# Half-height products turned into full-height ones: the last 64 hidden features of a transformer block's down projection

## The chip, the core and the metric

The kernel runs on one core of a Trainium2 chip. The metric is the device time of one execution in microseconds, the median of several runs. The profile is one separately taken execution of the same kernel; its times are counted from the start of its span.

## What is computed

A transformer block with adaptive layer norm, in float32, for two sequences of 1024 tokens with 256 features. The attention has 16 heads of 128 with rotary positions and a causal mask; the feed-forward part is gated, with 704 hidden features and weights given as integers with a scale per output.

```python
mod = (_silu(c) @ wmod).reshape(2, 6, 1, -1)
sa, ca, ga, sb, cb, gb = (mod[:, n] for n in range(6))
h = _layernorm(x) * (1 + ca) + sa
x = x + ga * attention(h)
h = _layernorm(x) * (1 + cb) + sb
gate = _silu(qlinear(h, wq_gate, s_gate))
up = qlinear(h, wq_up, s_up)
x = x + gb * qlinear(gate * up, wq_down, s_down)
```

(ga and gb are first kept at least 0.25 away from zero.) The change concerns the last line: the sum over the 704 hidden features.

## The kernel before

TensorE multiplies a stationary operand by a moving one; the dimension that is summed lies on the partitions, up to 128 of them, which are the rows of its array. 704 = 5 x 128 + 64, so the hidden features make NF = 6 chunks, five full ones and one of 64.

**Stages.** The kernel goes through 32 units (2 sequences x 16 heads). In each, the eight query tiles are scored, exponentiated, turned and multiplied with the values, and the projections of the next head are mixed in. The order is written out by hand in the loop at L753 and in `extras`, and the engines take their instructions in that order. The feed-forward part is done in four blocks of 512 tokens, named by sequence and half: (0,0), (0,1), (1,0), (1,1). The products of block (0,0) are mixed into the last attention unit, those of (0,1) into what is left of attention after it; the rest follows in the order of L813 to L830.

**One block.** `hidden(b, blk, c)` (L534) makes chunk c of the hidden features, transposed: features on the partitions, tokens along. It takes two products of TensorE (gate and up, L547), a Silu on ScalarE and a multiplication on VectorE, which writes the tile gT_b,blk (128 partitions x 6 chunks x 512 tokens). For the last chunk one product gives 64 gate features and 64 up features, and `last_gate_up` (L564) multiplies them. Its result is stored in two halves by token: of each 256 tokens, the first 128 (j even) go to partitions 0 to 63, and the other 128 (j odd) to partitions 64 to 127 (L573). The other half of the partitions of that chunk is written by nobody. `wq_down` is laid out to match: its last 64 rows are there twice, on partitions 0 to 63 and on 64 to 127 (L885).

`down(b, blk)` (L583) sums over the features. For each of four token tiles j there is an accumulator pd in PSUM, five products over the full chunks (`chunks`, L606) and one over the last chunk (`halves`, L596), which takes the 64 partitions that hold tile j. Then VectorE adds the residual (L622), and the DMA queue stores the rows (L623). In the first three blocks the halves come after all chunks; in the last block (1,1), whose chunk 5 is made first, they come before them. There the fourth token tile is split into two accumulators of 128 columns (pd and pd_11r).

**Buffers.** The gT tiles come from the pool `fpool` with two buffers: (0,0) and (1,0) use one, (0,1) and (1,1) the other. Before them, the same buffers hold the transposed layer norm of sequence 0, which GpSimd reads in `ln_shift` (L249) in the unit before the last. A tile's first writer waits until the last reader of the buffer's tile before it is done. The gate and up products after attention use the PSUM pool `ps_sc` with two buffers, each freed by the multiplication that reads it (L573, L581).

**GpSimd** does the rotary multiplications (L401, L407), the folding of the gates into the output weights (L339 to L343), the bias (L357) and the shifts of L249 during attention, and a few fills at the start. It has no work in the feed-forward blocks.

Of the kernel before, what the change touches and what calls it, by code (L numbers as in the profile page):

```python
# [11 lines left out]
F32 = mybir.dt.float32  # L12
# [5 lines left out]
P = 128  # L18
B, S, D = 2, 1024, 256
H, DH = 16, 128  # L20
HID = 704
# [4 lines left out]
NF = (HID + P - 1) // P  # L26
FULL = (HID // P) * P
QB = 512
# [9 lines left out]
def adaln_block(ctx: ExitStack, tc: tile.TileContext, a, cos_d, sin_d, out):  # L38
    nc = tc.nc
# [5 lines left out]
    fpool = pool("f", 2)  # L45
# [11 lines left out]
    cols = const.tile([P, 3 * H], F32, name="cols")  # L57
# [206 lines left out]
    wdT = [const.tile([P, NF, D], F32, name=f"wdT{b}") for b in range(B)]  # L264
# [240 lines left out]
    def bank(name):  # L505

        pool, tag = banks[turn[0] % 4]
        turn[0] += 1
        return pool.tile([P, 512], F32, tag=tag, name=name)
# [16 lines left out]
    h2s, gTs = {}, {}  # L526
# [6 lines left out]

    def hidden(b, blk, c, late=True, first=None, hold=False):  # L534
        if c == 0 if first is None else first:
            gTs[b, blk] = fpool.tile([P, NF, QB], F32, tag="f", name=f"gT_{b}{blk}")
        last = c == NF - 1
        if late:
            pg = ps_sc.tile([P, S], F32, tag="sc", name=f"pgu_{b}{blk}{c}")
            pgs = [pg[:, ts(j, QB)] for j in range(2)]  # L540
        else:
            pgs = [
                ps_a.tile([P, 512], F32, tag="a", name=f"pgu_{b}{blk}{c}{j}") for j in range(2 - last)
            ]
        for pg, n in zip(pgs, ("gate",) if last else ("gate", "up")):
            for k in range(KC):
                nc.tensor.matmul(  # L547
                    pg,
                    wT["last"][:, k, :] if last else wT[n][:, k, ts(c, P)],
                    h2s[b, blk][:, k, :],  # L550
                    start=(k == 0),
                    stop=(k == KC - 1),
                )
        sg = ppool.tile([P, QB], F32, tag="p", name=f"sg_{b}{blk}{c}")

        rest = (last_gate_up if last else full_gate_up)(b, blk, c, sg, pgs)
        if hold:
            owed.append(rest)
        else:
            rest()  # L560
# [22 lines left out]
    def down(b, blk):  # L583

        end = (b, blk) == (1, 1)
        pds = [bank(f"pd_{b}{blk}{j}") for j in range(4)]

        parts = [(j, pds[j], slice(0, D)) for j in range(4)]
        if end:
            rest = ps_sc.tile([P, S], F32, tag="sc", name=f"pd_{b}{blk}r")  # L590
            parts[3:] = [(3, pds[3], slice(0, P)), (3, rest, slice(P, D))]

        def halves():
            for j, pd, cols in parts:
                half = ts(j % 2, HID - FULL)
                nc.tensor.matmul(  # L596
                    pd[:, cols],
                    gTs[b, blk][half, NF - 1, ts(j, P)],
                    wdT[b][half, NF - 1, cols],
                    start=end,  # L600
                    stop=not end,
                )

        def chunks(j, pd, cols):
            for c in range(NF - 1):
                nc.tensor.matmul(  # L606
                    pd[:, cols],
                    gTs[b, blk][:, c, ts(j, P)],
                    wdT[b][:, c, cols],
                    start=(c == 0 and not end),  # L610
                    stop=(c == NF - 2 and end),
                )

        def store(j, pd, cols):
            t = blk * 4 + j
            if cols.start == 0:
                if (b, blk) == (0, 0):
                    yos[t] = rot.tile([P, D], F32, tag="r1", name=f"yo_{b}{t}")
                else:
                    yos[t] = xnp.tile([P, D], F32, tag="xn", name=f"yo_{b}{t}")  # L620
            yo = yos[t]
            nc.vector.tensor_tensor(yo[:, cols], pd[:, cols], x[b][:, t, cols], ALU.add)  # L622
            nc.sync.dma_start(out[b, ts(t, P), cols], yo[:, cols])  # L623

        yos = {}
        if end:

            halves()
            for part in parts:
                chunks(*part)  # L630
                store(*part)
            return
        for part in parts:
            chunks(*part)
        halves()
        for part in parts:
            store(*part)
# [62 lines left out]
    with tc.manual_schedule():  # L700
# [52 lines left out]
        for n, u in enumerate(units):  # L753
            b, g, h = u
# [4 lines left out]
            for i in range(NT):  # L759
# [20 lines left out]
                if not nxt and i in filler:  # L780
                    hidden(0, 0, filler.index(i), late=False, hold=True)
# [13 lines left out]
        for c in range(4):  # L795
            hidden(0, 1, c, hold=True)
            if c == 0:
                values(u, 0, 0, 4)
            for _ in range(2 + (c == 3)):
                shared_out(s, late=True)  # L800
                s += 1
            owed.pop()()
# [4 lines left out]
        values(u, 1, 0, 8)  # L807
        ln_scale(1, "b", 0)
        hidden(0, 1, 4)
        for t in range(4, NT):  # L810
            project_out(u, t, late=True)
# [85 lines left out]
```

## Time and profile before

| | |
|---|---|
| median of 3 runs | 1075.6 us (1075.38 to 1075.73) |
| profiled execution | 1076.84 us, of which the span is 1075.1 us |
| TensorE busy | 1070.5 us, 3529 records |
| VectorE / ScalarE / GpSimd busy | 655.1 / 507.7 / 396.1 us |
| granted TensorE clock | 1.00 |

| where in the profiled execution | us from the start |
|---|---|
| first product of the hidden layer written to gT_00 (L581) | 929.07 |
| last product of block (0,1)'s hidden layer, then layer norm | 991.03 to 993.62 |
| down product (0,0): full chunks, then halves | 993.62, 1002.35 |
| down product (0,1) | 1018.13, 1026.85 |
| down product (1,0) | 1045.38, 1054.10 |
| down product (1,1): halves, then full chunks | 1062.23, 1063.31 |
| last output addition | 1072.32 |

A line of the timeline gives the start, the length from the first record's start to the last one's end, the engine, the line of the code, the operation, the result and operands, the shape (for TensorE: rows * columns of the array, then rows x columns of what is streamed) and the number of records that were merged. PE is TensorE, PEld its weight loads, DVE VectorE, ACT ScalarE, POOL GpSimd, SPq the DMA queue. A float32 product leaves two records. The ends of TensorE's records are modelled, and so overlap with the next start; distances between starts are the safer measure.

### The profile page before, as it was taken

The page shows a single profiled execution, that of the slowest core. Times are in us where ns is not written, and L with a number is a line of the kernel's source. Part 1 is how long each engine was busy: PE and PEld are TensorE (multiplying, and loading weights), DVE is VectorE, ACT ScalarE, POOL GpSimd, SP SyncE. Part 2 cuts the span into 40 slices and gives each one's busy share as a digit, 9 for nine tenths or more (in the row PEclk, how much of TensorE's full clock was granted, in tenths as well). Part 3 has the DMA queues.
Part 4 walks back from the last instruction along what each step waited for, and adds up shares of the span by engine and source line. Part 5 has one row for each costly group of instructions (what it writes and reads, how often), then busy time and mean ns, then how long its engine had stood idle before and what let it go on. Part 6 is the DMA issues. An engine that isn't in the chain of part 4 may idle for free.

```text
span 1075.1 us, 12364 instructions
## 1 busy us (share of the span) xinstructions
PE 1070.5 (100%) x3529; PEld 641.4 (60%) x3529; DVE 655.1 (61%) x1423; ACT 507.7 (47%) x956; POOL 396.1 (37%) x364
## 2 busy tenths in 40 slices
PE   9999999999999999999999999999999999999998
PEld 5656555666666655555666656655555666555656
DVE  5656665666767776665666566666677765544421
ACT  4654544554445544544554444444454554562110
POOL 3825353534343343754332443324343433100000
PEclk9999999999999999999999999999999999999999
DMA  6465655657565555565554656454555556432001
GB/s 218 96 161 126 161 119 135 164 127 181 118 152 112 142 117 134 122 149 126 112 148 109 147 113 155 101 139 99 139 114 126 143 128 137 103 69 49 20 20 40
DMA packets 66656, 130.99 MB, mean 122 GB/s; under 512 B 18806, under 2 KB 22010, under 8 KB 66588
## 3 DMA queue, kind: packets, MB, share of 16 engines
q1 hardware_dynamic: 64804, 125.78, 49.4%
q10 hardware_dynamic: 1736, 4.29, 1.2%
q8 instruction: 29, 0.48, 0.2%
q14 instruction: 39, 0.32, 0.1%
q0 software_dynamic: 48, 0.13, 0.1%
HBM read 25.26 MB, written 2.10 MB: 25 GB/s over the span
## 4 chain that ended last, share of the span: by engine, by line
PE 99%; DMA 0%; DVE 0%; SPq 0%; issue 0%
PE po L492 23%; PE ps L431 23%; PE pv L370 10%; PE pq L388 10%; PE py L518 10%; PE pk L388 10%; PE pgu L547 7%; PE pd L606 3%; PE pm L125 1%; DMA wmod<-in_wmod 0%; PE pd L596 0%; PE ptx_a L218 0%; PE pg L149 0%; PE ptx_b L218 0%; PE pd_11r L606 0%; DVE x L521 0%
## 5 line engine op out<-in xcount | busy, mean ns | idle before, releaser
L451 ACT ACTIVATE p<-ps,nmax 128x128 f32<-128x128 f32 (+7 forms) x256 | 189.8, 741 | 342.7 <-DVE nmax L434 342.3
L431 PE MATMUL ps<-kT,qT 128*128 128x512 f32 (+3 forms) x768 | 289.5, 486 | 0.0
L434 DVE CUSTOM_DVE_ANT_0 ps<-ps,mask 128x128 f32<-128x128 f32 (+7 forms) x256 | 195.5, 764 | 114.5 <-PE ps L431 113.6
L492 PE MATMUL po<-pT,v 128*128 128x512 f32 (+3 forms) x768 | 263.7, 486 | 0.1
L521 DVE SCALAR_TENSOR_TENSOR x<-py,rden,x 128x256 f32<-128x256 f32 x256 | 122.7, 481 | 220.6 <-PE py L518 216.8
L492 PEld LDWEIGHTS po<-pT,v 128*128 128x128 f32 x768 | 145.7, 190 | 123.9 <-issue 92.8
L401 POOL TENSOR_TENSOR r_q<-r_q,sin_t 128x512 f32<-128x512 f32 x64 | 81.9, 1280 | 364.5 <-ACT r_q L400 348.9
L465 DVE STREAM_TRANSPOSE t<-p 128x128 f32<-128x128 f32 (+7 forms) x256 | 198.2, 774 | 3.6 <-DMA pT<-t 1.8
L431 PEld LDWEIGHTS ps<-kT,qT 128*128 128x128 f32 x768 | 145.7, 190 | 77.6 <-issue 64.1
L518 PE MATMUL py<-wo,o 128*128 128x256 f32 x512 | 151.2, 380 | 0.0
L518 PEld LDWEIGHTS py<-wo,o 128*128 128x128 f32 x512 | 92.6, 190 | 77.6 <-issue 53.1
L370 PE MATMUL pv<-wv,hT 128*128 128x256 f32 x512 | 121.1, 379 | 0.0
L388 PE MATMUL pq<-hT,wq 128*128 128x512 f32 x256 | 120.5, 593 | 0.0
L388 PE MATMUL pk<-hT,wk 128*128 128x512 f32 x256 | 120.3, 592 | 0.0
L370 PEld LDWEIGHTS pv<-wv,hT 128*128 128x128 f32 x512 | 94.8, 190 | 19.5 <-issue 1.3
L401 POOL TENSOR_TENSOR r_k<-r_k,sin_t 128x512 f32<-128x512 f32 x64 | 81.5, 1273 | 64.4 <-ACT r_k L400 64.4
L407 POOL TENSOR_TENSOR kT<-kT,r_k 128x512 f32<-128x512 f32 x64 | 81.2, 1269 | 55.8 <-DVE kT L404 41.1
L400 ACT ACTIVATE r_q<-pq,cols 64x512 f32<-64x512 f32 x128 | 87.4, 683 | 22.3 <-PE pq L388 19.8
L407 POOL TENSOR_TENSOR qT<-qT,r_q 128x512 f32<-128x512 f32 x64 | 83.7, 1308 | 33.9 <-DVE qT L404 29.7
L400 ACT ACTIVATE r_k<-pk,cols 64x512 f32<-64x512 f32 x128 | 87.4, 683 | 6.4 <-PE pk L388 1.0
L388 PEld LDWEIGHTS pk<-hT,wk 128*128 128x128 f32 x256 | 48.6, 190 | 48.0 <-issue 44.2
L388 PEld LDWEIGHTS pq<-hT,wq 128*128 128x128 f32 x256 | 46.2, 190 | 33.1 <-issue 30.6
(96 smaller groups left out, 691.3 us busy)
## 6 DMA issues: line engine op xcount, KB each, us to landing
pT<-t SPq DMA_DIRECT2D x512, 128.0 KB, 2.4
pT<-t SPq DMA_DIRECT2D x512, 64.0 KB, 2.0
wq<-in_Wq SPq DMA_DIRECT2D x16, 256.0 KB, 3.0
wk<-in_Wk SPq DMA_DIRECT2D x16, 256.0 KB, 4.1
wv<-in_Wv SPq DMA_DIRECT2D x16, 256.0 KB, 4.1
wo<-in_Wo SPq DMA_DIRECT2D x16, 256.0 KB, 2.9
out<-yo SPq DMA_DIRECT2D x15, 128.0 KB, 1.8
wmod<-in_wmod SPq DMA_DIRECT2D x4, 256.0 KB, 5.5
```

What stands on the lines that cost most here:

```text
L370: nc.tensor.matmul(pv[:, ts(j, HG * DH)], hT[b, n][:, k, ts(r, P)], weights[b, g]["v"][:, k, :], start=(k == 0), stop=(k == KC - 1),)
L388: nc.tensor.matmul(pq, weights[b, g][s][:, k, ts(h, DH)], hT[b, n][:, k, :], start=(k == 0), stop=(k == KC - 1),)
L400: nc.scalar.activation(r1[to], pq[of], AF.Identity, bias=cols[of, c : c + 1])
L401: nc.gpsimd.tensor_tensor(r1, r1, sin_t[:, sl], ALU.mult)
L407: nc.gpsimd.tensor_tensor(dst[:, sl], dst[:, sl], r1, ALU.add)
L431: nc.tensor.matmul(ps[:, c:e], qT[:, ts(i, P)], kT[:, c:e], start=True, stop=True)
L434: nc.vector.tensor_tensor_reduce(ps[:, :L], ps[:, :L], mask[:, NT - 1 - i :, :].rearrange("p t k -> p (t k)"), -SCALE, FLT_MAX, ALU.add, A ...
L451: nc.scalar.activation(p[:, :L], ps[:, :L], AF.Exp, bias=nmax, scale=-1.0, accum_out=dens[u][:, i : i + 1])
L465: nc.vector.transpose(t32[blk][:, :, j, : i + 1, :].rearrange("p c k b -> p k c b"), p[:, : (i + 1) * P].rearrange("p (k c a) -> p k c a", ...
L492: nc.tensor.matmul(po[:, off * P :], vs[b, g][:, k, ts(h, DH)], pT[:, off:, :, k, :], start=(k == 0), stop=(k == last),)
L518: nc.tensor.matmul(py[:, :D], outs[u][:, ts(t, P)], weights[b, g]["o"][:, h, :], start=True, stop=True)
L521: nc.vector.scalar_tensor_tensor(x[b][:, t, :], py[:, :D], rdens[u][:, t : t + 1], x[b][:, t, :], ALU.mult, ALU.add)
```

## The change

The last chunk's products no longer take the 64 partitions of their token tile but all 128. So that the other 64 add nothing, GpSimd writes zeros there: two fills for each gT tile, ahead of its first product. They clear partitions 64 to 127 of the even token tiles and 0 to 63 of the odd ones. What VectorE writes stays the same, and so do the weights, of which both copies are now read in each product. The number of products stays the same; their sum differs by nothing but products with zero.

```diff
     def hidden(b, blk, c, late=True, first=None, hold=False):
         if c == 0 if first is None else first:
-            gTs[b, blk] = fpool.tile([P, NF, QB], F32, tag="f", name=f"gT_{b}{blk}")
+            gT = gTs[b, blk] = fpool.tile([P, NF, QB], F32, tag="f", name=f"gT_{b}{blk}")
+
+            for j, rows_ in enumerate((slice(HID - FULL, P), slice(0, HID - FULL))):
+                nc.gpsimd.memset(
+                    gT[rows_, NF - 1, :].rearrange("p (t j q) -> p t j q", j=2, q=P)[:, :, j, :], 0.0
+                )
...
         def halves():
             for j, pd, cols in parts:
-                half = ts(j % 2, HID - FULL)
                 nc.tensor.matmul(
                     pd[:, cols],
-                    gTs[b, blk][half, NF - 1, ts(j, P)],
-                    wdT[b][half, NF - 1, cols],
+                    gTs[b, blk][:, NF - 1, ts(j, P)],
+                    wdT[b][:, NF - 1, cols],
                     start=end,
                     stop=not end,
                 )
```

## The prediction

> **What bounds the kernel now.** I read the page's busy table first, then the chain of waits for the stretch after attention, then TensorE's timeline around one down product, record by record, and last GpSimd's timeline. The busy table and the slices say which engine matters:
>
> ```profile
> PE 1070.5 (100%) x3529; PEld 641.4 (60%) x3529; DVE 655.1 (61%) x1423; ACT 507.7 (47%) x956; POOL 396.1 (37%) x364
> ...
> PE 99%; DMA 0%; DVE 0%; SPq 0%; issue 0%
> ```
>
> TensorE is busy in 1070.5 of 1075.1 us, and 99% of the chain that ended last is TensorE. So a nanosecond added to or taken from TensorE's stream is one of the end. The edited products are four places in the last 82 us; this is how TensorE's timeline lists one of them and its neighbours (start, length, records):
>
> ```profile
> 993.62 8.80 PE L606 MATMUL pd<-wdT,gT 128*128 128x256 f32 x40
> 1002.35 1.14 PE L596 MATMUL pd<-wdT,gT 64*128 64x256 f32 x8
> 1003.41 1.98 PE L547 MATMUL pgu<-h,wgateT 128*128 128x512 f32 x4
> 1005.23 1.88 PE L547 MATMUL pgu<-h,wupT 128*128 128x512 f32 x4
> ```
>
> Each fp32 product leaves two records, so the four half products (L596) are 8 records, and the twenty full ones (L606) 40. The lengths overlap, because the ends are modelled; what counts is the distance between starts. Cutting the window down to single records gives these starts (the first is the last L606 record, then four pairs of half-height records, then the first gate products):
>
> ```profile
> 1002.04 0.38 PE L606 MATMUL pd<-wdT,gT 128*128 128x256 f32 x1
> 1002.35 0.49 PE L596 MATMUL pd<-wdT,gT 64*128 64x256 f32 x2
> 1002.67 0.38 PE L596 MATMUL pd<-wdT,gT 64*128 64x256 f32 x2
> ...
> 1003.10 0.38 PE L596 MATMUL pd<-wdT,gT 64*128 64x256 f32 x2
> 1003.41 0.70 PE L547 MATMUL pgu<-h,wgateT 128*128 128x512 f32 x1
> 1003.95 0.59 PE L547 MATMUL pgu<-h,wgateT 128*128 128x512 f32 x1
> 1004.38 0.59 PE L547 MATMUL pgu<-h,wgateT 128*128 128x512 f32 x1
> ```
>
> Two things are to be seen. The half-height records come two at a time (x2 in one line at one start; a third pair starts at 1002.88): a product on rows 0 to 63 and one on rows 64 to 127 run together. And the steps are not even: 0.31, 0.32, 0.21, 0.22, 0.31, then 0.54 where the next is 0.43. The normal step of a 128x256 record is (1002.04 - 993.62)/39 = 0.216, and of a 128x512 record 0.43. So each change between full and half height costs about 0.1 on two steps: 0.09 + 0.10 going in and 0.10 + 0.11 coming out, 0.40 us for the four half products.
>
> **What the Trainium skill says.** "TensorEngine Tiling (Array Packing)", Key Properties, says that different tiles run in parallel, and that changing the tiling mode, as against the tile, drains TensorE. This trace agrees with both: four shared starts, and four stretched steps of 0.09 to 0.11 us. "TensorE: Matmul & The Clock Gate", in the section on LDWEIGHTS, says that a weight load's time depends on the columns and not on the rows; here 186 ns at 64 rows and 190 at 128, so the load itself won't grow. "SBUF — State Buffer", Who interferes with whom, says that a VectorE instruction with two SBUF inputs contends with GpSimd instructions that read SBUF, not with one that only writes. A fill only writes; no fill lies beside such VectorE work in this trace, so it is unverified here.
>
> **The change, part by part.**
>
> *Three down products with the half step last (starts 1002.35, 1026.85, 1054.10).* Removed: 4 pair steps and both changes of height. Added: 8 full-height records instead, which can't share the array. From the first L606 record to the end of the first gate group (four records), the trace has 1005.23 - 993.62 = 11.61; the second product has 1029.74 - 1018.13 = 11.61 and the third 1056.99 - 1045.38 = 11.61. After: 48 x 0.2159 + 4 x 0.4295 = 10.36 + 1.72 = 12.08 (0.4295 is a quarter of the 1.718 from one group of four to the next). Difference +0.47 each, 1.42 for three. By parts: 4 more steps of 0.216 cost +0.86, no changes of height -0.40.
>
> *The last down product (halves first, start 1062.23, two of its ten records 128 columns wide in each of pd and pd_11r).* Before: from the last up group's first record, 1060.42, to the first pd_11r record of the chunks, 1071.00, is 10.58. After: 4 x 0.4295 + 36 x 0.2159 + 14 x 0.112 = 1.72 + 7.77 + 1.57 = 11.06, the 36 being 6 halves and 30 chunk records of 256 columns, the 14 being 4 and 10 of 128 columns (0.112 from the starts of the last two output additions, 1071.20 and 1072.32, which are ten records apart). Difference +0.48. By parts: the narrow halves, all on rows 64 to 127, now run beside the two records of the third column block, so all ten records take four steps of 0.216, 0.86; alone they take 6 x 0.216 + 4 x 0.112 = 1.74. That is +0.88 for the lost pairing, and -0.40 for the changes of height.
>
> *Eight fills on GpSimd.* Each clears 64 rows of 256 words. The nearest row is a fill of 128 rows x 256 words before attention:
>
> ```profile
> 2.27 0.30 POOL L722 MEMSET bvacc<- 128x256 f32 x1
> ...
> 918.27 1.52 POOL L249 TENSOR_SCALAR h<-xt_b,modT 128x512 f32<-128x512 f32 x2
> ```
>
> So 0.3 each, 0.6 a pair, 2.4 in all. The second line is GpSimd's last work in the kernel: it ends at 919.79 and nothing is queued behind the fills, so their cost on GpSimd is nought. The first two pairs (gT_00, gT_01) come straight after it, because the buffers they take were last read by those same shifts: done near 921, against the first product written to gT_00 at 929.07. The pair of gT_10 must wait for the last reader of gT_00, the halves of the first down product: about 1004 to 1004.6 in the new order. The first VectorE write of gT_10 (L581), which now waits for it, starts at 1009.12: 4.5 us of cover. The pair of gT_11 starts after the second down product, near 1028.5, and the first write of gT_11 (L573) is at 1035.71: 6.6 us of cover. Behind such a write on VectorE stand the next gate products' multiplications, and TensorE waits for the PSUM buffers these release; if a pair took 5 us instead of 0.6, that would be the way to the end. I take nought. The bounds: below nought is excluded (the fills take no work from anyone), above I allow 0.5.
>
> *Waits added on TensorE.* The halves for the first two column blocks of each down product now also wait for GpSimd. These semaphores are up long before. A satisfied wait is not free by definition, so I look at like ones: in the first down product every column block's first L606 record waits for VectorE to free its bank, and its 39 steps still average 0.2159. I take nought; the bound above is 0.1 for each of the eight, 0.8, if a wait kept the weight load from running ahead, as at a change of height.
>
> *Moved.* Nothing else: the order on VectorE, ScalarE, the DMA queue and TensorE is the same, and no buffer changes. The output additions (L622) of a middle product come 0.2 to 0.5 later for the last two blocks; VectorE then has idle time until 1009.12.
>
> **Sum.** 1.42 + 0.48 = +1.90 us. The profiled execution took 1076.84 (span 1075.1 and 1.7 around it), so it would read 1078.7. It lies 1.24 above the median of the runs, 1075.6; the same step on the median gives 1077.5, +0.18%. About 0.2% (2.15 us, so 1077.75) is what a measurement of this kernel can tell from no change, and the forecast lies just under it.
>
> **The rivals.**
>
> *The stretched steps stay (slower).* I credit 0.40 per product to the change of height. If those tenths come from something else at the same places (the group of banks, the sequencer at a new line, the new waits on TensorE), they remain, and the cost is the lost pairing alone: 3 x 0.86 + 0.88 = +3.46, 1079.1. It decides from the point where more than 0.06 us of the 0.40 stays in each of the four places, because 1.90 + 0.25 passes the 0.2%. Against it: the stretch appears on both sides of the half rows in all four places, with L547 before, L606 after, or the other way round, while a change from L518 to L547 (989.30 to 991.03, eight records, 0.216 each) shows none.
>
> *The fills hold up VectorE (slower).* Needs a pair to end over 4.5 us after the halves. It would take GpSimd at some eight times the fill row's 0.30. It would give about +1 on top: 1078.5.
>
> *Part of the cost is absorbed.* TensorE has few holes in this stretch: one step at 1035.0 is 0.1 longer for a VectorE release, and the last additions and stores come after it anyway. At most half a microsecond to 1 us would vanish: 1076.6.
>
> *It doesn't do what it says (faster).* If full-height records of these products cost no more than a pair's share, 0.108, only the stretch goes: 4 x -0.40, 1074.0. L606, of the same shape, has 0.216 in all its steps, so nearly excluded.
>
> **How the numbers follow.** The forecast has 0.66: its own range is 1077.0 to 1078.1, with measurement of the two medians (the runs spread 0.35) and the small bounds; 0.17 of the 0.66 lies above 1077.75. The stretch staying 0.18, fills 0.05, absorbed 0.08, no cost 0.03. So slower by over 0.2%: 0.17 + 0.18 + 0.05 = 0.40; within: 0.49 + 0.08 = 0.57; faster 0.03. The range runs from 1076.7, in the absorbed case, to 1079.2, just past the rival of the stretch.
>
> **What would show it.** In the profile after: L596 as 128-row records in steps of 0.216, no stretched step before or behind them, 12.08 between the two starts named above; right for the pairing and wrong for the stretch if that reads about 12.5. Eight fills of 0.3 on GpSimd near 920, 1004 and 1028. Wrong altogether if L581 at about 1009 or L573 at about 1036 waits for GpSimd, or if any L606 or L596 step waits for it.

## The result

| | before | after |
|---|---|---|
| median of 10 runs each | 1075.73 us | 1078.26 us |
| lowest to highest | 1075.38 to 1077.58 | 1077.30 to 1079.80 |
| ratio of after to before | | 1.0018, 95% interval 1.001 to 1.0026 |
| profiled execution (span) | 1076.84 (1075.1) us | 1079.60 (1077.8) us |

0.18% is what was forecast, and it is clear of nought. The two medians are 2.5 us apart, the two lowest runs 1.92. Both kernels have runs in two groups, about 1.5 us apart, and the median of ten falls in one or the other, or between them, by chance; a large part of what makes the groups is found below. The span of after's profiled execution is 2.7 us longer, but 0.9 of that is there before the first down product starts (994.52 instead of 993.62). The rest lies behind it: from the first record of the first down product to the first chunk record of pd_11r, near the end, TensorE takes 1071.00 - 993.62 = 77.38 us before and 1073.76 - 994.52 = 79.24 after, 1.86 more. This distance is called the changed stretch below.

**The stretch that was changed.** TensorE's timeline of after, at the place shown before, and the same from the last full-height record on, cut down to single records. The new half step is L600 now, the full chunks are L610 and the gate products L552:

```profile
994.52 8.80 PE L610 MATMUL pd<-wdT,gT 128*128 128x256 f32 x40
1003.15 1.89 PE L600 MATMUL pd<-wdT,gT 128*128 128x256 f32 x8
1004.88 1.88 PE L552 MATMUL pgu<-h,wgateT 128*128 128x512 f32 x4
1006.60 1.88 PE L552 MATMUL pgu<-h,wupT 128*128 128x512 f32 x4
```

```profile
1002.94 0.38 PE L610 MATMUL pd<-wdT,gT 128*128 128x256 f32 x1
1003.15 0.38 PE L600 MATMUL pd<-wdT,gT 128*128 128x256 f32 x1
...
1004.67 0.38 PE L600 MATMUL pd<-wdT,gT 128*128 128x256 f32 x1
1004.88 0.59 PE L552 MATMUL pgu<-h,wgateT 128*128 128x512 f32 x1
```

One record stands at each start now, where there were two. The step from L610 to L600 is 0.21 (it was 0.31), seven steps take 1003.15 to 1004.67, 0.217 each, and the step to the gate products is 0.21 (0.31). The gate group takes 1.72 again instead of 1.82. From 994.52 to 1006.60 it is 12.08 us, the forecast number to the last digit; the second and third product have 1031.57 - 1019.49 = 12.08 and 1059.28 - 1047.20 = 12.08. In the last one, from the up group at 1062.71 to pd_11r at 1073.76, it is 11.05, where 11.06 was forecast.

**The fills.** GpSimd's timeline of after, its last work before them and all eight:

```profile
919.18 1.52 POOL L249 TENSOR_SCALAR h<-xt_b,modT 128x512 f32<-128x512 f32 x2
920.76 1.38 POOL L539 MEMSET gT<- 64x256 f32 x4
1005.16 0.67 POOL L539 MEMSET gT<- 64x256 f32 x2 [83.02 <-PE pd L600]
1030.13 0.66 POOL L539 MEMSET gT<- 64x256 f32 x2 [24.30 <-issue]
```

They stand where they were expected, and a pair takes 0.67. VectorE's first write to gT_10 comes at 1010.55, 0.1 after ScalarE's result as before. No step of TensorE in this stretch is held up by GpSimd.

**The 0.9 us ahead of it.** The chain of waits of after has an entry that the one of before lacks, a load of the down scales. In order of time, around it (start, length, what):

```profile
247.32 8.50 DMA s_down<-in_scales
...
255.85 1.28 DVE sd L296
...
257.76 0.49 DVE x L521
...
258.29 0.70 PE py L518 x2
```

The load is issued at 247.3 and lands 8.5 us later; VectorE waits 2.8 us for it, and an addition to x (L521) that frees TensorE's accumulator stands behind. TensorE's timeline shows 1.47 us of idle time ahead of the product at 258.29. Before's trace has the same load landing in 7.4 us; VectorE waits 1.6 us there and TensorE loses nothing. Record by record, after falls 1.90 us behind before at this place (the idle time and the longer steps behind it). Up to here it had been 1.00 ahead, because before had lost time in its first 20 us: its sixteen `pm` records (L125) take 3.54 us, from 6.79 to 10.33, where after's take 1.86, from 6.69 to 8.55; why wasn't tried. The 0.9 is the difference of the two. The changed lines are far from this place, so this looked like chance, and q_before and q_after below try it.

### The profile page after: what moved, and what is told of

It is laid out like the page before. It is cut to its first block, busy times and chain, and to the rows that moved or that the text cites. A ratio compares the mean times of both kernels' runs of the same rounds, so it can differ in the third digit from the quotient of the medians.

```text
span 1077.8 us, 12378 instructions
## 1 busy us (share of the span) xinstructions
PE 1071.3 (99%) x3529; PEld 642.5 (60%) x3529; DVE 656.6 (61%) x1423; ACT 507.6 (47%) x956; POOL 398.6 (37%) x372
## 4 chain that ended last, share of the span: by engine, by line
PE 98%; DMA 1%; DVE 0%; ACT 0%; issue 0%; SPq 0%; ACTq 0%
PE ps L431 23%; PE po L492 23%; PE pk L388 10%; PE py L518 10%; PE pq L388 10%; PE pv L370 10%; PE pgu L552 7%; PE pd L610 3%; DMA s_down<-in_scales 1%; PE pd L600 1%; DMA wmod<-in_wmod 0%; PE pm L125 0%; PE ptx_a L218 0%; PE pg L149 0%; PE ptx_b L218 0%; DVE x L521 0%
## 5 line engine op out<-in xcount | busy, mean ns | idle before, releaser
L521 DVE SCALAR_TENSOR_TENSOR x<-py,rden,x 128x256 f32<-128x256 f32 x256 | 122.6, 481 | 220.4 <-PE py L518 216.7
```

The source lines that it names most:

```text
L521: nc.vector.scalar_tensor_tensor(x[b][:, t, :], py[:, :D], rdens[u][:, t : t + 1], x[b][:, t, :], ALU.mult, ALU.add)
```

## The experiments

My theory: the whole cost is TensorE's, the lost pairing of products (+0.86 to 0.88 for each down product) less the changes of height (0.40 each). The rivals: fills or waits have a share; the stretched steps belong to something other than the height.

**e1: the fills alone.** Only the first part of the diff, `halves` as before.

> The eight fills alone: half-height products as before. My theory (the cost is all in TensorE's products): no change, within 0.3 us of before, and 11.61 us from the first full record of each of the first three down products to the end of the first gate group behind it, as before. The rival (the fills or the waits for them cost something): 0.3 to 1 us longer, with VectorE or TensorE waiting for GpSimd in the stretch after 929 us.

Measured: 1076.23 us against 1076.61 for before beside it, ratio 0.9997 (0.9989 to 1.0005). TensorE's timeline of this kernel:

```profile
992.74 8.80 PE L611 MATMUL pd<-wdT,gT 128*128 128x256 f32 x40
1001.47 1.13 PE L601 MATMUL pd<-wdT,gT 64*128 64x256 f32 x8
1002.53 1.98 PE L552 MATMUL pgu<-h,wgateT 128*128 128x512 f32 x4
```

992.74 to 1002.53 is 9.79, as before (993.62 to 1003.41). The fills cost nothing that shows; the changed stretch is 77.38 us here too.

**e2: full-height products without fills.**

```diff
+                    gTs[b, blk][:, 0, ts(j, P)],
+                    wdT[b][:, 0, cols],
```

> Full-height products without any fill: the last step of a down product reads chunk 0 a second time in place of chunk 5, so chunk 5 is left out of the result. My theory: all of the change's cost, +1.9 us against before, 12.08 us in each of the first three places. The rival (fills and waits have a share): less than +1.6.

Measured: 1077.89 us, ratio 1.0016 (1.0009 to 1.0023); the lowest runs are 1077.20 and 1075.21. TensorE's timeline of this kernel:

```profile
992.13 8.80 PE L605 MATMUL pd<-wdT,gT 128*128 128x256 f32 x40
1000.76 1.89 PE L595 MATMUL pd<-wdT,gT 128*128 128x256 f32 x8
1002.49 1.88 PE L547 MATMUL pgu<-h,wgateT 128*128 128x512 f32 x4
1004.21 1.88 PE L547 MATMUL pgu<-h,wupT 128*128 128x512 f32 x4
```

From the first full record, 992.13, to the end of the first gate group, 1004.21, it is 12.08. With e1 this settles where the cost is: the products have all of it, the fills and their waits none.

**e3: half height without pairs.** What the two parts of my sum rest on is that pairing and change of height are different things. Here all four products take the same rows.

```diff
-                half = ts(j % 2, HID - FULL)
+                half = slice(0, HID - FULL)
...
-                    gTs[b, blk][half, NF - 1, ts(j, P)],
-                    wdT[b][half, NF - 1, cols],
+                    gTs[b, blk][half, 0, ts(j, P)],
+                    wdT[b][half, 0, cols],
```

> Half-height products, but all four on rows 0 to 63, so that no two can run together; they read the first 64 features of chunk 0 in place of chunk 5, whose features are left out. Theory A (the 0.40 us of stretched steps belongs to the change of height): pairing lost and stretch kept, 12.48 us in each of the first three places and +3.5 us in all. Theory B (the stretch comes with two products running together): no pair, no stretch, 12.08 us and +1.9 us.

Measured: 1080.11 us, ratio 1.0031 (1.0019 to 1.0042), so +3.3 from the ratio; +3.5 between the lowest runs (1078.74 and 1075.21).

```profile
992.60 8.80 PE L606 MATMUL pd<-wdT,gT 128*128 128x256 f32 x40
1001.33 1.99 PE L596 MATMUL pd<-wdT,gT 64*128 64x256 f32 x8
1003.25 1.98 PE L547 MATMUL pgu<-h,wgateT 128*128 128x512 f32 x4
1005.07 1.88 PE L547 MATMUL pgu<-h,wupT 128*128 128x512 f32 x4
```

992.60 to 1005.07 is 12.47: theory A's 12.48, and not B's 12.08. Unpaired half-height products are dearer than full-height ones by just the two changes of height, 12.47 - 12.08 = 0.39.

**e4: twice as many changes of height.**

```diff
-        for part in parts:
-            chunks(*part)
-        halves()
+        for two in (parts[:2], parts[2:]):
+            for part in two:
+                chunks(*part)
+            halves(two)
```

> As before, but in the first three down products the half steps are made in two visits of two products each, after the second and after the fourth token tile, with full-height chunks between. Theory A (each change of height costs 0.2 us): one more change out and back in each of three products, 12.01 us from the first full record to the end of the gate group instead of 11.61, +1.2 us in all. Theory B (the stretch is a cost of each product at its end, or of the line of code that changes): 11.61 us, no change.

Measured: 1077.65 us, ratio 1.0010 (1.0002 to 1.0019); lowest runs 1076.41 and 1075.21, +1.2.

```profile
993.24 4.48 PE L606 MATMUL pd<-wdT,gT 128*128 128x256 f32 x20
997.65 0.70 PE L596 MATMUL pd<-wdT,gT 64*128 64x256 f32 x4
998.28 4.58 PE L606 MATMUL pd<-wdT,gT 128*128 128x256 f32 x20
1002.80 0.70 PE L596 MATMUL pd<-wdT,gT 64*128 64x256 f32 x4
1003.43 1.99 PE L547 MATMUL pgu<-h,wgateT 128*128 128x512 f32 x4
1005.25 1.88 PE L547 MATMUL pgu<-h,wupT 128*128 128x512 f32 x4
```

993.24 to 1005.25 is 12.01, as theory A has it: 0.40 for one more visit, with neither end of the product nor a gate product beside it. The cost goes by change of height. A change of line or of accumulator alone doesn't bring it: in after, the same change of both, from L610 to L600, has a step of 0.21. The middle entry of the timeline shows it by itself: twenty full records from 998.28 to 1002.80 take 4.52, where 20 x 0.216 is 4.32.

**e5: fills sixteen times over**, for the tiles of the second sequence, in the changed kernel.

```diff
+                for _ in range(16 if b else 1):
                     nc.gpsimd.memset(
```

> The changed kernel with each fill of the second sequence's tiles made sixteen times over, so that a pair takes about 10.7 us instead of 0.67. If VectorE's first write to a tile waits for the fills and TensorE in turn for the PSUM buffers, as the prediction said: the fills of gT_10 end near 1015.8, VectorE's write that stood at 1010.5 starts there, and TensorE loses up to 1 us there and about 2 us behind gT_11, so 1 to 3 us over the changed kernel. If only the last step of the down product waits for the fills: no change against the changed kernel.

Measured: 1077.93 us, 1.0018 (1.0011 to 1.0024) of before, like the changed kernel. GpSimd's fills and VectorE's first write to gT_10 in its timelines:

```profile
1003.59 11.54 POOL L540 MEMSET gT<- 64x256 f32 x32 [83.02 <-PE pd L601]
```

```profile
1008.98 0.69 DVE L587 TENSOR_TENSOR gT<-sg,pgu 128x512 f32<-128x512 f32 x1 [3.56 <-POOL gT L540]
```

The fills end at 1015.1, and VectorE writes at 1008.98 all the same: 5.67 after the gate group's start at 1003.31, as in after (1010.55 - 1004.88). The label on this line names GpSimd, but the write starts 0.1 after ScalarE's result, which ends at 1008.88. So, against what I had said, the first write doesn't wait for the whole pair; which of GpSimd's instructions the wait is for, the trace doesn't tell. It is the same with gT_11: its fills run from 1028.51 to 1040.05, and VectorE's first write to it starts at 1034.25. The down product's last step, which does need the pair, starts at 1054.27, 39 us after the first pair's end. The changed stretch is 79.24 us, as in after.

**q_before and q_after: the load of the down scales earlier.** The load moves from the end of unit 7 to the end of unit 6, and its use from query tiles 1, 3, 5 to 3, 5, 7.

```diff
+        if n == 6 and i == 7:
+            ffn_down_scale_load()
         if n == 7 and i == 7:
             ffn_down_load()
-        if n in (8, 9) and i in (1, 3, 5):
-            ffn_down_scale(n - 8, i - 1)
+        if n in (8, 9) and i in (3, 5, 7):
+            ffn_down_scale(n - 8, i - 3)
```

> The kernel before, with the load of the down scales issued one unit earlier and the scaling of the down weights two query tiles later. The profile after shows a chain through that load near 255 us and 1.5 us of TensorE idle behind it; the profile before shows a wait for it too, without idle TensorE. If that wait is what spreads the runs by 2 us: all runs within about 0.5 us of each other, near 1075.5. If it isn't: the same spread as before.

> The changed kernel with the same two moves (load of the down scales a unit earlier, their use two query tiles later). If the wait for that load spreads the runs: all within about 0.5 us of each other, near 1077.4, and 1.9 us over the kernel before with the same moves. If the change has a cost of its own beyond 1.9 us: more than 2.3 us over it.

Measured: q_before 1075.58 us (1075.24 to 1076.88, 13 runs) and q_after 1077.61 (1077.05 to 1078.76, 21 runs), beside before with 1075.96 (1075.33 to 1078.82, 51 runs). In neither trace does anything wait for the load. Of before's runs 18 of 51 lie more than 1 us above the lowest, of q_before's 2 of 13, of q_after's 4 of 21. So this wait has a large part in the upper group, but not every high run comes from it; the spread did not shrink to 0.5 us, as expected, but to 1.6 and 1.7. The traces of the kernels without the two moves agree: TensorE loses 1.90 us behind this load in after, 1.46 in e8, 0.14 and 0.19 in e5 and e6, and nothing in the other five. The distance between the two medians is 2.0 us, between the two lowest runs 1.8, so no cost of the change shows besides the 1.9.

**e6: one visit for two products (missed).** If a visit costs 0.40, two down products can share one: the half steps of the first stand directly ahead of those of the second, which takes its accumulators from `ps_sc`. Core of the new order:

```diff
+        for part in parts[0]:
+            chunks(0, *part)
+        halves(0)
...
+            halves(1)
...
+        for part in parts[1]:
+            chunks(1, *part)
+            store(1, *part)
```

> Half-height products as before, but the two down products of a sequence stand one behind the other, the half steps of the first directly ahead of those of the second (the second takes its accumulators from the PSUM pool of the hidden products). Two of the four visits to half height are left. Theory A (0.40 us a visit): 0.8 us shorter than before, and only two stretched groups in TensorE's steps. Theory B (no cost by visit): no change. Either way some wait on the output additions could come up at the new place and take it back.

Measured: 1079.17 us, ratio 1.0031 (1.002 to 1.0042), 3 us longer.

```profile
992.60 8.80 PE L600 MATMUL pd<-wdT,gT 128*128 128x256 f32 x40
1001.33 2.00 PE L590 MATMUL pd<-wdT,gT 64*128 64x256 f32 x16
1003.25 2.43 PE L600 MATMUL pd<-wdT,gT 128*128 128x256 f32 x10
1007.14 4.58 PE L600 MATMUL pd<-wdT,gT 128*128 128x256 f32 x20 [1.47 <-DVE yo L616]
1012.25 2.42 PE L600 MATMUL pd<-wdT,gT 128*128 128x256 f32 x10 [0.52 <-DVE yo L616]
```

The sixteen half records have one visit, as meant. What came up is a new wait: two token tiles lie in one PSUM tile, and the products of the second wait for the addition that reads the first. There are four such stops in the two sequences, 1.47 us and three times 0.52 of idle time. With the longer steps at them they cost 1.74 and three times 0.79, 4.1 us together; less the 0.8 saved, that leaves the 3.3 us by which the changed stretch is longer than before's (80.67).

**e8: the same without that wait.** The additions come after both products of a PSUM tile.

```diff
-        for part in parts[1]:
-            chunks(1, *part)
-            store(1, *part)
+        for some in (parts[1][:2], parts[1][2:4], parts[1][4:]):
+            for part in some:
+                chunks(1, *part)
+            for part in some:
+                store(1, *part)
```

> The two down products of a sequence one behind the other as in the run with one visit, but the output additions of two token tiles that share a PSUM tile are made after the products of both, so that no product waits for an addition. Theory A (0.40 us a visit to half height, two of four visits gone): 0.8 us shorter than before, 9.79 + 9.79 - 0.40 = 19.2 us for the two products of sequence 0 together, and no TensorE wait for an output addition. Theory B (what the earlier run lost was not those waits): still 2 us or more longer than before.

Measured: 1075.07 us against 1075.91 for before beside it, ratio 0.9991 (0.9983 to 0.9999), -0.84.

```profile
994.21 8.80 PE L600 MATMUL pd<-wdT,gT 128*128 128x256 f32 x40
1002.94 2.00 PE L590 MATMUL pd<-wdT,gT 64*128 64x256 f32 x16
1004.87 8.90 PE L600 MATMUL pd<-wdT,gT 128*128 128x256 f32 x40
1013.61 1.88 PE L547 MATMUL pgu<-h,wgateT 128*128 128x512 f32 x4
```

No wait for an addition is left. The two products take 1013.61 - 994.21 = 19.40, not the 19.2 that I had written down: my sum used the distance to the first gate record, 9.79, which leaves out the second stretched step of the way back. With it, two products took 2 x 9.90 before, and 19.40 is 0.40 less. The changed stretch, with all four products, runs from 994.21 to 1070.80: 76.59 us, 0.79 less than before's.

**e9: both.**

> The same, with the load of the down scales a unit earlier and their use two query tiles later. If both hold: 0.8 us under the kernel before with those moves alone (1075.58), so 1074.8, with runs within about 1 us of each other.

Measured: 1074.82 us (1074.45 to 1075.25, 21 runs), 0.9987 (0.998 to 0.9993) of before. None of the 21 runs lies more than 1 us above the lowest; of the 33 of before beside them, 15 do. This version beats both kernels, by a little: half-height pairs kept, two visits instead of four, and no wait for the scales.

## Why the prediction held

*TensorE sets the end.* Right. The 1.9 us of the four places stand in the end unchanged, 1.92 between the lowest runs and 2.0 between q_after and q_before. The changed stretch shows it without the spread of the runs: 77.38 us in before, e1 and q_before, 79.24 in after, e2, e5 and q_after (+1.86), 80.80 in e3 (+3.42), 78.58 in e4 (+1.20), 76.59 in e8 (-0.79).

*The number.* Its closeness is in part luck. The interval of the ratio, 0.10 to 0.26%, would have held anything from 1.1 to 2.8 us and spans the 0.2% that the prediction names. The measured median, 1078.26, lies 0.8 above the 1077.5 and just above the forecast's own range of 1077.0 to 1078.1, because half of after's ten runs fell in the upper group. What was foreseen is the +1.9 in TensorE's steps.

*Lost pairing, +0.86 and +0.88.* Right: eight records at eight starts, 0.217 apart, one by one.

*Changes of height, -0.40.* Right, and the term that the forecast hung on: without it the sum is +3.46. e3 keeps the changes and loses the pairs (12.47), after loses both (12.08), e4 adds a change back and forth (+0.40), e8 takes two visits away (-0.84 in all). That the array drains at a change of height, as the Trainium skill says in "TensorEngine Tiling (Array Packing)", Key Properties, fits this; the traces show the price, not the draining. They do show that the weight load of the first half-height record starts together with its product, at 1002.35 in before, while the load of a full one starts a step ahead (1001.83 for the product at 1002.04). One thing I had overlooked: two longer steps like these also stand behind stops with no change of height, 0.16 and 0.10 in before at 945.16, behind a wait for ScalarE, and 0.10 and 0.11 at 933.51, behind one for VectorE, with the weight load beside its product again. So a change of height costs here about what a short stop of the stream costs.

*Fills at nought.* Right in size: e1 costs nothing, and the pair took 0.67 where 0.6 was estimated. The reason was partly wrong. I took VectorE's first write to gT_10 to wait for the pair, with 4.5 us of cover; e5's pair of 11.54 us held up nothing, so the cover is larger, reaching to the down product's last step.

*Added waits at nought.* Right: e2, without fills and without those waits, has the same 12.08 as after.

*Absorbed in part.* Not so: the step near 1036 that VectorE stretches by 0.1 is there after as before.

*What I hadn't seen.* The wait for the scales' load at 255 us. It stood in before's trace too, as 1.6 us of VectorE's idle time, and in after's trace it costs as much as the change does. My step of 1.24 us from the profiled execution to the median doesn't come from there, for TensorE lost nothing at that place in before's trace. It fits what before lost in its first 20 us: between there and the load, all the other traces run 0.4 to 1.5 us ahead of before's.

## What to carry to other kernels

When the summed dimension leaves a half chunk, two half-height products on different rows share the array, but each visit to half height is paid for at both ends; gather the half-height products into few visits, and compare what pairing saves with that. Here a visit with four products saves 0.86 us and pays 0.40. On a stream that sets the end, distances between starts predicted each place of this edit to a hundredth of a microsecond; TensorE's busy times, 1070.5 and 1071.3 us, whose ends are modelled, show 0.8 of the 1.9. Before reading a difference of 0.2% from medians, look at whether the runs lie in groups, and find the wait that makes them.

## What the runs showed of the hardware

- A change from full to half height and back costs 0.39 to 0.40 us here, in four steps that are each 0.09 to 0.11 longer, two behind each change; with pairs and without, at 256 columns and beside 512.
- Unpaired half-height records take the same step as full-height ones (e3: 0.39 above after, all of it from the changes), so half the rows save nothing by themselves.
- A fill of 64 rows x 256 words on GpSimd takes 0.33 to 0.36 us, one of 128 rows x 256 words took 0.30: half the rows took no less time. The 64-row fill lies in two pieces of 128 words; what that costs wasn't tried.
- The first VectorE instruction on the scales (sd, L296 in after) took 1.27 us in after's profile and 0.43 in before's. In the four traces where it starts while a GpSimd instruction runs (after, q_before, q_after, e9) it takes 0.91 to 1.27 us and ends 0.28 to 0.29 after that instruction (256.84 and 257.12 in after); in the eight others it takes 0.42 to 0.43. That fits VectorE waiting for GpSimd there; no run tried it by itself. It makes 0.84 us of after's delay behind the load.
